# Causal attention beside a ternary FFN: the products with V of two key chunks made in one visit at every second chunk

## The chip, the cores and the metric

The kernel runs on one core of one Trainium2 chip. The metric is the device time of one execution in microseconds (µs). Three runs of the kernel before gave 2402.01, 2408.93 and 2418.55 µs; the median is 2408.93.

## The reference

The input `x` is 4 batches of 2048 tokens with 256 features. It is normalised over the features, and two branches read the result. The attention branch has 16 heads of 16 features, rotary positions on q and k, and a causal mask; the FFN branch (256 to 1024 and back) rounds its weights to three values and ends in a silu. The output is `x` plus the product of the branches.

```
xn  = layernorm(x)
q, k, v = xn @ Wq.T + bq, xn @ Wk.T + bk, xn @ Wv.T + bv     # 16 heads of 16
q, k = apply_rope(q), apply_rope(k)
att = softmax(where(tril, q @ k.T / 4, -inf))
s   = (att @ v) @ Wo.T + bo
g   = silu(gelu(xn @ ternary(W1).T + b1) @ ternary(W2).T + b2)
out = x + s * g
```

## The kernel before, in words

**Tiling.** Queries are taken in 16 blocks of 512 (`blk`; 4 blocks in each batch, `n = blk % 4`), and the heads in 4 groups of 4 (`g`). A group of a block attends to the keys in chunks of 128. Block `n` has `4 * (n + 1)` chunks, called units here and `kb` in the code, so that a group has 4, 8, 12 or 16 units. The last four units of a group lie on the diagonal and are narrower: 512, 384, 256 and 128 queries. In all there are 64 groups and 640 units.

**The three kinds of attention work on TensorE.** They are short visits, and the text names them by letters:
- **M**, in `maxima` (L686): the scores of the *next* group, queries as output rows, two matmuls into two PSUM banks (L704; on the diagonal a mask is added by L717). VectorE then takes the row maxima of each bank, one `tensor_reduce` per bank (L727, or L731). These maxima are needed one group later.
- **S**, in `scores` (L779): the scores of one chunk and one pair of heads (`j` is 0 or 1), transposed, four matmuls (L791, keys first and then the maxima to be taken off) into two neighbouring banks. ScalarE takes the exponentials of both in one instruction (L798) into a buffer `e` of pool `pp`; on the diagonal GpSimd clears what the mask forbids (L802).
- **V**, in `times_v` (L813): the weighted sum with V of one chunk, four heads side by side in four strips of 32 output columns (L815), eight matmul records in the trace, accumulated in PSUM bank 7 over the whole group.

M and S matmuls use the array in halves of 64 rows (`64*128` in the profile), V uses it in strips of 32 columns (`128*32`), and projections, transposes and FFN use it whole (`128*128`).

**The banks.** Seven PSUM banks are handed out in the order in which they were given back (`bank` at L98, `two_banks` at L103, `release` at L113). The handing out is done while the program is written, not on the chip: the next M or S gets the bank whose last user stands furthest back in the program, and on the chip its matmul waits until that user's reduce or exponential has read the bank. `two_banks` takes, of all free neighbouring pairs, the one whose later member is oldest.

**The order of the work** is written out by the loop from L1092 on. For each unit it advances `values` (L772) by two steps with `next(steps)`, and before each step it lets `maxs.to` (L1124, L1127) make M visits in proportion to the work done, about one per step. A step ends at a `yield`. Before the change, a unit is therefore M, S, S, then M, V, where V is that of the chunk before (`pending`). After the second step come, where there are any, one action of `ends` (in the first unit of a group: the last two V of the group before, and the copy of bank 7 to `av_sb`, L842 to L863), parts of the projection of a later block (`proj`) and deferred steps of the block's end (`finish`). The FFN (`feed`, L566) runs between groups.

**The loads.** Keys, queries and values of a group are loaded by the queue of SyncE (L656, L663, L671). The class `Loads` (L615) counts free buffers: 3 for q, 8 for k, 5 for v. A key tile holds 512 keys; a group of block `n` has `n + 1` of them, and while a group is worked on, M needs those of the next one too.

Of the kernel before, what the change touches and what calls it, by code (L numbers as in the profile page):

```python
# [26 lines left out]
GH = H // G  # L27
# [11 lines left out]
def attention_gated_by_ffn(  # L39
# [63 lines left out]
    def two_banks(name):  # L103
        when = {i: k for k, i in enumerate(free_banks)}
        i = min(
            (i for i in when if i + 1 in when), key=lambda i: max(when[i], when[i + 1])
        )
        free_banks.remove(i)
        free_banks.remove(i + 1)
        taken.setdefault(name, []).append([i, i + 1])  # L110
        return psum[:, i : i + 2, :]

    def release(name):  # L113
        free_banks.extend(taken[name].pop(0))
# [36 lines left out]
    sels = [const.tile([P, P], F32R, name=f"sel{j}") for j in range(GH // 2)]  # L151

    xp = ctx.enter_context(tc.tile_pool(name="xp", bufs=1))
    kp = ctx.enter_context(tc.tile_pool(name="kp", bufs=8))
    vp = ctx.enter_context(tc.tile_pool(name="vp", bufs=5))
    qp = ctx.enter_context(tc.tile_pool(name="qp", bufs=3))
    work = ctx.enter_context(tc.tile_pool(name="work", bufs=2))
# [1 line left out]
    small = ctx.enter_context(tc.tile_pool(name="small", bufs=2))  # L159
    yp = ctx.enter_context(tc.tile_pool(name="yp", bufs=2))  # L160
    hp = ctx.enter_context(tc.tile_pool(name="hp", bufs=4))
    pp = ctx.enter_context(tc.tile_pool(name="pp", bufs=4))
    tp = ctx.enter_context(tc.tile_pool(name="tp", bufs=4))

    def setup():
# [449 lines left out]
    class Loads:  # L615


        def __init__(self):
            self.free = {"q": 3, "k": 8, "v": 5}
            self.next = {  # L620
                "q": iter(groups),
                "k": iter([(*x, c) for x in groups for c in range(x[0] % NQ + 1)]),
                "v": iter([(*x, c) for x in groups for c in range(x[0] % NQ + 1)]),
            }
            self.head = {k: next(i) for k, i in self.next.items()}
            self.ahead = {"q": 2, "k": 2, "v": 1}
            self.now = 0
# [144 lines left out]
    def values(blk, g):  # L772

        n = blk % NQ
        mT, q = mTs.pop((blk, g)), qst[blk, g]
        last = (n + 1) * TT - 1
        pending, exs = [], {}

        def scores(kb, j, q0):  # L779
            s2 = two_banks("s2")  # L780
            w = NB - q0

            at = NB - 2 * P if kb == last else 0
            if not at:
                exs[j] = pp.tile([P, 2, NB], F32, tag="e", name="e")
            e = exs[j][:, :, at : at + w]
            for part in range(2):
                for a in range(2):
                    rows = slice(a * ST, (a + 1) * ST)
                    k = kst[blk, g, kb // TT][rows, j, (kb % TT) * P : (kb % TT + 1) * P]  # L790
                    nc.tensor.matmul(  # L791
                        s2[:, a, :w],
                        (k, sels[j][rows, :])[part],
                        (q[rows, j, q0:], mT[rows, q0:])[part],
                        start=(part == 0),
                        stop=(part == 1),
                    )
            nc.scalar.activation(e, s2[:, :, :w], AF.Exp, scale=1.0 / math.sqrt(HD))  # L798
            release("s2")
            if kb >= n * TT:  # L800

                nc.gpsimd.affine_select(  # L802
                    out=e[:, :, :P],
                    in_=e[:, :, :P],
                    pattern=[[0, 2], [1, P]],
                    compare_op=ALU.is_ge,
                    fill=0.0,
                    base=0,
                    channel_multiplier=-1,
                )  # L810
            return e

        def times_v(kb, ex, q0):  # L813
            for h in range(GH):
                nc.tensor.matmul(  # L815
                    av[h * HP : (h + 1) * HP, q0:],
                    vst[blk, g, kb // TT][:, kb % TT, h * VE : h * VE + HP],
                    ex[h // 2][:, h % 2, : NB - q0],
                    start=(kb == 0),
                    stop=(kb == last),  # L820
                )
            if kb % TT == TT - 1:
                vst.pop((blk, g, kb // TT))
                loads.release("v")

        for kb in range(last + 1):
            q0 = max(kb - n * TT, 0) * P
            ex = [scores(kb, j, q0) for j in range(GH // 2)]
            if kb % TT == TT - 1:
                kst.pop((blk, g, kb // TT))  # L830
                loads.release("k")
            yield
            if kb < last:
                while pending:
                    times_v(*pending.pop())
            pending.append((kb, ex, q0))
            yield
        qst.pop((blk, g))

        def end():  # L840
            for chunk in pending:
                times_v(*chunk)  # L842
            av_sb = one.tile([P, NB], F32, tag="av_sb", name="av_sb")
            nc.scalar.copy(av_sb, av)
            if g == 0:
                ys[blk] = yp.tile([P, KC, NB], F32, tag="y", name="y")
                ws[blk] = small.tile([P, H * NB // P], F32, tag="w", name="w")

            tail = blk == NBLK - 1
            for h in range(GH):  # L850
                d = (g * GH + h) * HD
                queue = nc.scalar if tail and g == G - 1 else nc.sync
                queue.dma_start(
                    out=ys[blk][d % P : d % P + HD, d // P, :],
                    in_=av_sb[h * HP : h * HP + HD, :],
                )
                a = (g * GH + h) * P // H
                nc.sync.dma_start(
                    out=ws[blk][a : a + P // H, :],
                    in_=av_sb[h * HP + HD : h * HP + HD + 1, :].rearrange(  # L860
                        "o (a k) -> o a k", a=P // H
                    ),
                )  # L863
            if tail and g >= G - 2:

                if g == G - 2:
                    last_steps.extend(finish(blk))
                for _ in range(last_steps.index(None) if g == G - 2 else len(last_steps)):
                    deferred.append(last_steps.pop(0))
            elif g == G - 1:  # L870
                deferred.extend(finish(blk))

        ends.append(end)
# [193 lines left out]
    with tc.manual_schedule():  # L1067
# [24 lines left out]
        for i, (blk, g) in enumerate(groups):  # L1092
# [22 lines left out]
            if fast:  # L1115
                for k, _ in enumerate(gate):
                    past += slots.pop(0) if k < FC else 0

                    if k % 3 == 2:
                        maxs.to(past / whole)  # L1120
            steps = values(blk, g)
            for u in range(units):
                past += slots.pop(0)
# [84 lines left out]
```

## Time and profile before

| | µs |
|---|---|
| median of three runs | 2408.93 |
| span of the profiled execution (first to last instruction) | 2397.2 |
| profiled execution's own time: 11.2 before the first instruction, and the span | 2408.4 |
| PE (matmuls) busy | 2269.8 (95%) |
| DVE (VectorE) busy | 1620.1 (68%) |
| ACT (ScalarE) busy | 1472.5 (61%) |
| POOL (GpSimd) busy | 886.6 (37%) |
| mean granted TensorE clock | 0.986 of full |

How to read the profile: a matmul's record lasts from its start to the end of its results, and matmuls follow each other faster than that, so PE can be "busy" all the time and still wait. The distance from one start to the next is what a matmul costs in a stream. "PEld" is the load of the stationary operand, which can run ahead of the matmul; a wait for a bank is often shown there. In the list of waits a line reads: who waited, for whom, µs in total, times, and the longest. In the timeline a line reads: start, µs, engine, line, operation, output and inputs, array tiling, moving shape, how many records are merged, and in brackets the idle time before it and who ended it.

### The profile page before, as it was taken

The page shows a single profiled execution, that of the slowest core. Times are in us where ns is not written, and L with a number is a line of the kernel's source. Part 1 is how long each engine was busy: PE and PEld are TensorE (multiplying, and loading weights), DVE is VectorE, ACT ScalarE, POOL GpSimd, SP SyncE. Part 2 cuts the span into 40 slices and gives each one's busy share as a digit, 9 for nine tenths or more (in the row PEclk, how much of TensorE's full clock was granted, in tenths as well). Part 3 has the DMA queues.
Part 4 walks back from the last instruction along what each step waited for, and adds up shares of the span by engine and source line. Part 5 has one row for each costly group of instructions (what it writes and reads, how often), then busy time and mean ns, then how long its engine had stood idle before and what let it go on. Part 6 is the DMA issues. An engine that isn't in the chain of part 4 may idle for free.

```text
span 2397.2 us, 43912 instructions
## 1 busy us (share of the span) xinstructions
PE 2269.8 (95%) x16852; PEld 1222.7 (51%) x16852; DVE 1620.1 (68%) x2910; ACT 1472.5 (61%) x1889; POOL 886.6 (37%) x1262
## 2 busy tenths in 40 slices
PE   5799999999999999999999999999999999999997
PEld 4554545545455455544545454455554545455443
DVE  9656677775556676696636768768663766777881
ACT  4554656656766565765766565565676646566665
POOL 2136343235443535315344542522525453431000
PEclk8889999999999999999999999999999999999998
DMA  7344335234253524234234443412514352442311
GB/s 222 113 135 161 92 127 157 58 104 136 75 165 118 178 86 159 79 91 145 67 127 128 151 142 111 155 56 86 176 58 140 120 179 79 135 140 62 88 46 32
DMA packets 247617, 280.38 MB, mean 117 GB/s; under 512 B 108784, under 2 KB 143728, under 8 KB 247408
## 3 DMA queue, kind: packets, MB, share of 16 engines
q1 hardware_dynamic: 243680, 271.95, 35.7%
q10 hardware_dynamic: 3728, 5.64, 0.7%
q8 instruction: 132, 2.16, 0.4%
q14 instruction: 77, 0.63, 0.1%
HBM read 181.08 MB, written 87.52 MB: 112 GB/s over the span
## 4 chain that ended last, share of the span: by engine, by line
PE 71%; DVE 10%; ACT 7%; POOL 6%; issue 3%; DMA 2%; SPq 1%; ACTq 0%; DVEq 0%; POOLq 0%
PE psum L791 19%; PE psum L815 19%; PE psum L704 14%; PE psum L600 5%; PE psum L513 3%; PE psum L581 3%; DVE mx L727 3%; ACT e L798 3%; DVE mx L731 2%; PE psum L539 2%; PE psum L953 2%; PE psum L717 2%; ACT mT L765 1%; POOL qklo L397 1%; ACT g L608 1%
## 5 line engine op out<-in xcount | busy, mean ns | idle before, releaser
L727 DVE TENSOR_REDUCE mx<-psum 128x1 f32<-128x512 f32 (+1 forms) x2048 | 1258.2, 666 | 497.1 <-PE psum L704 350.1
L798 ACT ACTIVATE e<-psum 128x1024 f32<-128x1024 f32 (+3 forms) x1280 | 1081.3, 894 | 630.4 <-PE psum L791 596.0
L704 PE MATMUL psum<-kst,qst 64*128 64x512 f32 (+3 forms) x2560 | 613.0, 421 | 27.1 <-ACT h L592 9.3
L815 PE MATMUL psum<-e,vg 128*32 128x512 f32 (+3 forms) x5120 | 596.5, 543 | 15.7 <-POOL e L802 15.5
L802 POOL TENSOR_SCALAR_AFFINE_SELECT e<-e 128x256 f32<-128x256 f32 x512 | 208.0, 416 | 1001.0 <-ACT e L798 972.2
L791 PE MATMUL psum<-qst,kst 64*128 64x512 f32 (+3 forms) x2560 | 554.6, 395 | 22.3 <-DVE mx L727 5.7
L704 PEld LDWEIGHTS psum<-kst,qst 64*128 64x128 f32 x2560 | 309.0, 185 | 449.4 <-DVE mx L727 287.9
L791 PE MATMUL psum<-mT,sel 64*128 64x512 f32 (+3 forms) x2560 | 516.8, 370 | 6.0 <-ACT mT L765 3.2
L791 PEld LDWEIGHTS psum<-qst,kst 64*128 64x128 f32 x2560 | 285.1, 185 | 171.9 <-ACT e L798 55.4
L791 PEld LDWEIGHTS psum<-mT,sel 64*128 64x128 f32 x2560 | 273.3, 186 | 43.7 <-ACT mT L765 24.1
L594 POOL TENSOR_TENSOR hl<-h,hh 128x512 fp32r<-128x512 f32 x128 | 164.9, 1298 | 149.9 <-ACT h L592 114.3
L815 PEld LDWEIGHTS psum<-e,vg 128*32 128x32 f32 x5120 | 109.9, 108 | 161.0 <-issue 112.4
L731 DVE TENSOR_REDUCE mx<-psum 128x3 f32<-128x384 f32 x256 | 130.3, 552 | 57.7 <-PE psum L717 53.3
L592 ACT ACTIVATE hh<-psum,b1c 128x512 fp32r<-128x512 f32 x128 | 88.4, 691 | 80.4 <-PE psum L581 80.2
L513 PE MATMUL psum<-xf,wqkvT 128*128 128x512 f32 x256 | 125.9, 616 | 0.9 <-ACT xf L458 0.9
L717 PE MATMUL psum<-mask_k,mask_q 64*128 64x64 bf16 (+1 forms) x1536 | 121.1, 205 | 0.0
L600 PE MATMUL psum<-hh,w2T 128*128 128x512 f32 x256 | 107.1, 418 | 0.2 <-ACT w2T L367 0.2
L581 PE MATMUL psum<-xh,w1T 128*128 128x512 f32 x256 | 104.8, 409 | 0.6 <-POOL xh L396 0.5
L581 PE MATMUL psum<-xl,w1T 128*128 128x512 f32 x256 | 103.1, 403 | 0.8 <-POOL xl L397 0.8
L600 PE MATMUL psum<-hl,w2T 128*128 128x512 f32 x256 | 102.3, 399 | 0.2
L521 ACT ACTIVATE qk<-psum,bqk 128x512 f32<-128x512 f32 x64 | 44.0, 689 | 86.4 <-PE psum L513 85.9
L592 ACT ACTIVATE h<-psum,b1c 128x512 f32<-128x512 f32 x128 | 87.9, 687 | 0.0
(135 smaller groups left out, 1635.9 us busy)
## 6 DMA issues: line engine op xcount, KB each, us to landing
kst<-kd SPq DMA_DIRECT2D x160, 512.0 KB
qst<-qd SPq DMA_DIRECT2D x64, 512.0 KB
vg<-vd SPq DMA_DIRECT2D x160, 166.0 KB
qd<-qkhi SPq DMA_DIRECT2D x32, 512.0 KB
qd<-qklo SPq DMA_DIRECT2D x32, 512.0 KB
kd<-qkhi SPq DMA_DIRECT2D x30, 512.0 KB
kd<-qklo SPq DMA_DIRECT2D x30, 512.0 KB
vd<-v SPq DMA_DIRECT2D x16, 574.0 KB
```

What stands on the lines that cost most here:

```text
L513: nc.tensor.matmul(pq, wqkvT[:, kc, at : at + P], xf[:, kc, :], start=(kc == 0), stop=(kc == KC - 1),)
L581: nc.tensor.matmul(ph, w1T[:, kc, f * P : (f + 1) * P], x12[:, kc, :], start=(kc + i == 0), stop=(kc + i == KC),)
L592: nc.scalar.activation(to, ph, AF.Gelu, bias=b1c[:, f : f + 1])
L600: nc.tensor.matmul(pgs[dc], w2T[:, f - 2, dc * P : (dc + 1) * P], hx, start=(f - 2 + i == 0), stop=(f - 2 + i == FC),)
L704: nc.tensor.matmul(s1[:, at : at + wt], q[rows, j, t * P : (t + 1) * P], kst[blk, g, c][rows, j, :wt], start=(at == 0), stop=(c < n),)
L717: nc.tensor.matmul(to[:, :, i * ST : (i + 1) * ST], mask_q[rows, i, :], mask_k[rows, i, : len(ts), :], start=False, stop=(i == 1),)
L727: nc.vector.tensor_reduce(mx[:, 2 * j + a, at : at + 1], s1[:, :w], AX.X, ALU.max)
L731: nc.vector.tensor_reduce(mx[:, 2 * j + a, at : at + w // P], s1[:, :w].rearrange("p (b k) -> p b k", k=P), AX.X, ALU.max,)
L791: nc.tensor.matmul(s2[:, a, :w], (k, sels[j][rows, :])[part], (q[rows, j, q0:], mT[rows, q0:])[part], start=(part == 0), stop=(part == 1),)
L798: nc.scalar.activation(e, s2[:, :, :w], AF.Exp, scale=1.0 / math.sqrt(HD))
L802: nc.gpsimd.affine_select(out=e[:, :, :P], in_=e[:, :, :P], pattern=[[0, 2], [1, P]], compare_op=ALU.is_ge, fill=0.0, base=0, channel_mult ...
L815: nc.tensor.matmul(av[h * HP : (h + 1) * HP, q0:], vst[blk, g, kb // TT][:, kb % TT, h * VE : h * VE + HP], ex[h // 2][:, h % 2, : NB - q0 ...
```

## The change

Three things are changed.
1. In `values`, V is no longer made in every unit for the chunk before. At every even `kb` the products of both pending chunks are made, one after the other in their order; at an odd `kb` there are none.
2. So that each unit still has two steps, an odd unit gives control back between its two S: its order becomes M, S, M, S. An even unit is M, S, S, then M, V, V.
3. The pool `pp` of the exponentials has six buffers in place of four (4 KB per partition each), and the pool `kp` of the keys six in place of eight (4 KB each); the count in `Loads` follows.

The last two chunks of a group are still made together in the first unit of the next group, and nothing changes in what is computed.

```
-    kp = ctx.enter_context(tc.tile_pool(name="kp", bufs=8))
+    kp = ctx.enter_context(tc.tile_pool(name="kp", bufs=6))
...
-    pp = ctx.enter_context(tc.tile_pool(name="pp", bufs=4))
+    pp = ctx.enter_context(tc.tile_pool(name="pp", bufs=6))
...
-            self.free = {"q": 3, "k": 8, "v": 5}
+            self.free = {"q": 3, "k": 6, "v": 5}
...
         for kb in range(last + 1):
             q0 = max(kb - n * TT, 0) * P
-            ex = [scores(kb, j, q0) for j in range(GH // 2)]
+            ex = [scores(kb, 0, q0)]
+            if kb % 2:
+                yield
+            ex.append(scores(kb, 1, q0))
             if kb % TT == TT - 1:
                 kst.pop((blk, g, kb // TT))
                 loads.release("k")
             yield
-            if kb < last:
+            if kb % 2 == 0:
                 while pending:
-                    times_v(*pending.pop())
+                    times_v(*pending.pop(0))
+                yield
             pending.append((kb, ex, q0))
-            yield
         qst.pop((blk, g))
```

## The prediction

> **What bounds the kernel now.** First the page's busy shares and the chain that ended last:
>
> ```profile
> PE 2269.8 (95%) x16852; PEld 1222.7 (51%) x16852; DVE 1620.1 (68%) x2910; ACT 1472.5 (61%) x1889; POOL 886.6 (37%) x1262
> ...
> PE 71%; DVE 10%; ACT 7%; POOL 6%; issue 3%; DMA 2%; SPq 1%; ACTq 0%; DVEq 0%; POOLq 0%
> ```
>
> TensorE looks like the bound. But a matmul record contains its latency, so the second view is the timeline of PE in a stretch without projections (block with n = 3):
>
> ```profile
> 1392.78 0.86 PE L815 MATMUL psum<-e,vg 128*32 128x256 f32 x16
> 1393.56 0.50 PE L704 MATMUL psum<-kst,qst 64*128 64x512 f32 x2
> 1394.24 0.50 PE L791 MATMUL psum<-qst,kst 64*128 64x512 f32 x2 [0.18 <-ACT e L798]
> ...
> 1396.59 0.50 PE L704 MATMUL psum<-kst,qst 64*128 64x512 f32 x2
> 1397.07 0.51 PE L791 MATMUL psum<-qst,kst 64*128 64x512 f32 x2
> 1397.41 0.40 PE L791 MATMUL psum<-mT,sel 64*128 64x512 f32 x2
> 1397.65 0.39 PE L791 MATMUL psum<-qst,kst 64*128 64x512 f32 x2
> 1397.87 0.40 PE L791 MATMUL psum<-mT,sel 64*128 64x512 f32 x2
> 1398.11 0.39 PE L704 MATMUL psum<-kst,qst 64*128 64x512 f32 x2
> 1398.43 1.07 PE L815 MATMUL psum<-e,vg 128*32 128x512 f32 x8
> 1399.42 0.50 PE L704 MATMUL psum<-kst,qst 64*128 64x512 f32 x2
> ```
>
> One unit is 1396.59 to 1399.42, 2.83 us. By starts: a pair of half-array matmuls costs 0.23 (1397.65 to 1397.87), so M is 0.23 and S 0.46. M costs 0.32 ahead of V (1398.11 to 1398.43) and 0.34 behind it (1399.42 to the next S at 1399.76). V costs 0.99. Without waits a unit is 0.34 + 0.92 + 0.32 + 0.99 = 2.57; 0.26 is waiting, most of it hidden in the records. For whom, the third and fourth views say (waits; then ACT, DVE and PE rows, and the groups by shape):
>
> ```profile
> ACT e L798 <- PE psum L791: 596.0, 604, 4.9
> DVE mx L727 <- PE psum L704: 350.1, 299, 8.5
> PEld psum L704 <- DVE mx L727: 287.9, 433, 3.4
> PEld psum L815 <- POOL e L802: 21.3, 30, 1.6
> ```
>
> ```profile
> 1393.17 1.02 ACT L798 ACTIVATE e<-psum 128x1024 f32<-128x1024 f32 x1
> 1397.91 1.94 ACT L798 ACTIVATE e<-psum 128x1024 f32<-128x1024 f32 x2 [0.89 <-PE psum L791]
> 1423.82 0.73 PE L704 MATMUL psum<-kst,qst 64*128 64x512 f32 x4
> 1424.35 1.29 DVE L727 TENSOR_REDUCE mx<-psum 128x1 f32<-128x512 f32 x2 [5.17 <-PE psum L704]
> L727 DVE TENSOR_REDUCE mx<-psum 128x1 f32<-128x512 f32 x1792 | 1129.6, 683 | 441.6 <-PE psum L704 350.1 <-PE psum L717 73.8 <-PE psum L791 3.1
> L798 ACT ACTIVATE e<-psum 128x1024 f32<-128x1024 f32 x896 | 870.9, 1022 | 401.8 <-PE psum L791 391.2 <-issue 3.7 <-POOL xh L396 2.6
> ```
>
> The reader is to see that each engine waits for the other through the seven banks. S at 1394.24 starts 0.05 after the exponential that read its bank (1393.17 + 1.02 = 1394.19). So a bank comes back at these ages. **A bank of M:** the first reduce starts 0.53 after M (1423.82 to 1424.35), lasts 0.69, the second starts 0.60 later (1.29 - 0.69): with 0.05 for the release the banks are free 1.27 and 1.87 after M's start. **A bank of S:** results are ready when the second pair ends (1397.65 to 1398.27) and the exponential starts 0.1 later, 0.72 after S; 1.02 long, 0.05 release: free 1.79 after S's start.
>
> **What the change takes away.** A group of U units has U - 1 V visits before and U/2 after: 3, 7, 11, 15 become 2, 4, 6, 8, so 576 become 320, 256 fewer. A V visit of 512 columns takes 0.99; the one at 1392.78 holds two chunks of 256 and 128 columns and takes 0.78. So a column costs 0.21/128 = 1.65 ns, a visit 0.15 beside its columns, and two full chunks in one visit 1024 x 1.65 ns + 0.15 = 1.85. With the M before (0.32 for 0.23) and the M behind (0.34 for 0.23) a visit less saves 0.15 + 0.09 + 0.11 = 0.35. All 256: 90 us, the most that PE can win.
>
> The Trainium skill, "TensorEngine Tiling (Array Packing)", says under Key Properties that changing the tiling mode drains TensorE, which is this 0.35; by that alone the time would be 2408 - 90 = 2318. Its section PSUM Bottleneck speaks against: tiling makes TensorE faster but not the emptying of PSUM; by that none of the 90 need arrive. The rows above decide for the second, and the sum below goes by them.
>
> **What it moves.** I followed the list of free banks through both programs. Before, an S nearly always gets a bank with a V between its last user and itself. After, in the 192 full-width odd units that have another odd unit behind them, the second S (S1) gets a bank of the M just ahead of the first S (call it Ma) in 144, and the bank of the first S itself (S0) in 20; only one S and one M, or one M, lie between. In the even unit behind, the second S (S1') gets the bank of S1 in nearly all, with one M and one S between. So two latencies that V used to cover lie bare in each pair of units, while V, V comes as one lump in which DVE and ACT run dry.
>
> Priced from Ma's start at 0: S0 at 0.34, second M (Mb) at 0.80, S1 could start at 1.03. It starts at 1.27 (Ma's first bank), 1.87 (second bank) or 0.34 + 1.79 = 2.13 (S0's). S1' starts 1.79 later at the earliest: 3.06, 3.66 or 3.92; unhindered it would be S1 + 1.15. Where the S before it (S0') gets Mb's second bank, that is free at 0.53 + 3 x 0.60 + 0.69 + 0.05 = 3.07, and S1' comes at 3.53 at the earliest. Behind S1' stand S 0.46, M 0.32 and V, V 1.85: 2.63 to the next Ma. Pairs: 5.69, 6.16, 6.29, 6.55.
>
> *133 full-width pairs without projection work* (measured now: mean 5.84). 31 have first bank and then Mb's second (6.16), 39 second bank (6.29), 20 first bank throughout (5.69), 17 S0's (6.55), 9 no M at all (4.25 as now), 17 other mixtures (6.2): mean 6.05. Now, the commonest sort of pair has a floor near 5.54 and a mean of 5.92, since other work of DVE and ACT (the 0.59 copy to av_sb, sums, statistics) comes between. The new chain runs through the same two engines. Bounds: none of the 0.38 or all, 6.05 to 6.43; I take half, 6.25. So +0.41 x 133 = **+55** (28 to 78).
>
> *59 full-width pairs with projection work* (now 7.79). Work between S1 and the next M covers S1', work behind V, V covers nothing: PE work 4.81 (M 0.92, S 1.84, V 1.85, switches 0.20) and a stall of 0.84, or 6.05, plus the visit; a projection visit of 1.91 gives 7.56 or 7.96 where 7.55 is seen now. 0 to +0.6, I take 0.35: **+21** (0 to 35).
>
> *64 narrow pairs on the diagonal.* The same with shorter reduces (0.55) and exponentials (0.81): some 0.4 x 64 = 26 lost. Against it V waits less for GpSimd's masking, since the chunk just masked is the second of the visit or comes two units later: at most the 21 of the list above, I take 16. **+10** (-15 to 30).
>
> *Buffers.* Six for exponentials suffice: a pair's buffers come back with the V, V ahead of the S that needs them; nothing waits. With six key tiles, the key loads with 8 or more units between issue and first M fall from 138 to 75 of 160, and most of the rest have 4 or 5. Four units are 11 us; 512 KB take 2.3 to 4.5 us at the page's 222 and 117 GB/s. SP's queue can delay them: six come three units behind a store of projections that waits for POOL (up to 9.1 us in SP's waits). 0 to 30, I take **+5**.
>
> FFN, first block and group ends keep their order: 0. Sum: 55 + 21 + 10 + 5 = **+91**; bounds +13 and +173. Against the profiled execution's own 2408.4 (its span 2397.2 and 11.2 ahead; 0.5 under the median of the runs) this makes 2500, between 2421 and 2581.
>
> **Rivals.**
> *TensorE is the bound and wins.* For it: 95% busy, 71% of the chain, and 287.9 us of PEld waits for DVE that a V, V might let DVE catch up with. Against: the ages of the banks. It decides if S1 starts within 0.1 of 1.03 behind Ma. Price: -0.35 x 256 = -90, 2318; with half of it, 2363. Chance 0.10.
> *Both cancel.* If nearly all S1 wait for the first bank only (0.24) and S0' hides the rest, pairs are 5.69 for 5.84: -20 + 21 + 5, about 2415. Chance 0.08.
> *The keys come late.* For it: 4 units of lead where there were 8 or more. If a load took over 11 us, two a group would wait in 16 long groups, some 3 us each: +96 on top, about 2595. Against: 2.3 to 4.5 us. Chance 0.07.
> *The forecast*: 0.75.
>
> **Numbers.** 2500. Faster by over 1% 0.10, within 1% 0.08, slower 0.82; 1% is about what a measurement of this kernel can tell. The range reaches from 2424, above the cancelling case, to 2575: left out are 0.10 + half of 0.08 below and some 0.06 above.
>
> **What would show it.** 320 V visits, the two-chunk ones at 1.85. PE busy falls below 92%, DVE and ACT gain share in the chain. PEld L791 waits for DVE rise from 31.9 us in 59 times to some 80 in over 120, and for ACT from 55.4 in 160 by some 70. V's waits for POOL shrink to a few us. M's waits for the key loads stay under 20. I am wrong if S1 follows Mb at 0.23 in most odd units, if the pairs at full width without projections stay under 5.8, or if DMA waits carry the loss.

## The result and the profile after

The changed kernel takes 2507.06 µs (median of four runs, 2504.78 to 2509.78), against 2407.07 for the kernel before on the same chip: a ratio of 1.0412 with a 95% interval of 1.038 to 1.0443. It is slower by some 100 µs, where +91 (2500) was forecast. The profiled spans are 2502.8 and 2397.2: 105.6 apart. Two of the ten executions of one kernel below (the changed kernel with half maxima) were disturbed, 3880 and 10874 µs; its median leaves them out, and its trace, which is of the first, is not read.

The page of the changed kernel, the lines that answer to those shown of before (busy shares and chain), with the group of the first matmuls of S (keys) of its fifth part, and under it the same group of the kernel before:

```profile
PE 2320.7 (93%) x16852; PEld 1239.3 (50%) x16852; DVE 1601.9 (64%) x2910; ACT 1486.1 (59%) x1889; POOL 882.5 (35%) x1262
...
PE 67%; DVE 15%; ACT 11%; issue 3%; DMA 1%; POOL 1%; SPq 1%; ACTq 0%; DVEq 0%; POOLq 0%
...
L791 PE MATMUL psum<-qst,kst 64*128 64x512 f32 (+3 forms) x2560 | 704.4, 418 | 103.2 <-ACT e L798 53.3
```

```profile
L791 PE MATMUL psum<-qst,kst 64*128 64x512 f32 (+3 forms) x2560 | 554.6, 395 | 22.3 <-DVE mx L727 5.7
```

Two things are to be seen. The chain lost 4 points on PE and gained 5 on DVE and 4 on ACT. And "busy" misleads: PE is busy for 51 µs more with the same 16852 matmuls, because waits that are short enough disappear inside the records: the row at 501.32 below, 1.09 long where 0.39 is usual, holds one. The first matmuls of S were 554.6 µs busy before and are 704.4 now, with 103.2 of visible idle time where there were 22.3.

The list of waits of the changed kernel (who waited, for whom: µs in total, times, longest):

```profile
ACT e L798 <- PE psum L791: 690.4, 612, 7.7
DVE mx L727 <- PE psum L704: 450.0, 299, 6.3
PEld psum L791 <- DVE mx L727: 157.0, 364, 1.7
PEld psum L791 <- ACT e L798: 129.6, 211, 1.4
PEld psum L704 <- DVE mx L727: 114.8, 217, 3.3
PEld psum L815 <- POOL e L802: 17.7, 53, 1.1
PE psum L815 <- POOL e L802: 0.6, 4, 0.2
```

In the list of the kernel before, S (L791) had:

```profile
PEld psum L791 <- ACT e L798: 55.4, 160, 0.8
PEld psum L791 <- DVE mx L727: 31.9, 59, 1.0
```

S now waits for reduces 364 times in place of 59 and for exponentials 211 times in place of 160; ACT and DVE in turn idle 94 and 100 µs more for want of scores. M (L704) waits less for reduces than before, 114.8 µs in place of 287.9.

A pair of units at full width shows how. As in the prediction, Ma, S0, Mb, S1 are the visits of the odd unit, and S0' and S1' the two S of the even unit behind it; Mc is the M between S1 and S0'. The timelines of PE, then DVE and ACT, of the changed kernel, in a group of a block with n = 3:

```profile
500.04 0.50 PE L704 MATMUL psum<-kst,qst 64*128 64x512 f32 x2
500.38 0.39 PE L791 MATMUL psum<-qst,kst 64*128 64x512 f32 x2
...
500.84 0.39 PE L704 MATMUL psum<-kst,qst 64*128 64x512 f32 x2
501.32 1.09 PE L791 MATMUL psum<-qst,kst 64*128 64x512 f32 x2
501.92 0.73 PE L791 MATMUL psum<-mT,sel 64*128 64x512 f32 x2
502.26 0.39 PE L704 MATMUL psum<-kst,qst 64*128 64x512 f32 x1
...
503.12 0.50 PE L791 MATMUL psum<-qst,kst 64*128 64x512 f32 x1 [0.23 <-DVE mx L727]
...
503.82 0.49 PE L791 MATMUL psum<-qst,kst 64*128 64x512 f32 x2
504.16 0.40 PE L791 MATMUL psum<-mT,sel 64*128 64x512 f32 x2
504.39 0.39 PE L704 MATMUL psum<-kst,qst 64*128 64x512 f32 x2
504.71 1.92 PE L815 MATMUL psum<-e,vg 128*32 128x512 f32 x16
506.57 0.49 PE L704 MATMUL psum<-kst,qst 64*128 64x512 f32 x2
```

```profile
500.57 3.68 DVE L727 TENSOR_REDUCE mx<-psum 128x1 f32<-128x512 f32 x6 [1.12 <-PE psum L704]
...
501.10 1.03 ACT L798 ACTIVATE e<-psum 128x1024 f32<-128x1024 f32 x1 [1.96 <-PE psum L791]
502.74 1.03 ACT L798 ACTIVATE e<-psum 128x1024 f32<-128x1024 f32 x1 [0.62 <-PE psum L791]
```

Ma stands at 500.04. The second S of the odd unit (S1) could start at 501.07 and starts at 501.32, its second pair only at 501.92: its two banks are Ma's, and Ma's two reduces end 1.22 and 1.82 after Ma. S0' gets its second bank at 503.12 (the fourth of the six reduces). S1' starts at 503.82, which is 0.05 after the exponential of S1 (502.74 + 1.03 = 503.77). Then V, V takes 1.86 (504.71 to 506.57) as one block. In the V, V just ahead of this pair DVE and ACT had run dry: they stand idle for 1.12 and 1.96 before their first work for it (500.57 and 501.10). The pair lasts 6.53; the same pair of the kernel before lasts 5.85.

**Where the 105.6 µs are.** From the first matmuls of S in both traces, by stretches: 133 plain full-width pairs 5.84 to 6.58 each, +98; 59 full-width pairs with projection work 7.79 to 8.25, +27; the 64 narrow pairs +4; a group's first unit -3; from a group's last unit to the next group -20. The sum is +106.

### The profile page after: what moved, and what is told of

Read it like the earlier page. It is cut to its first block, busy times and chain, and to the rows that moved or that the text cites. A ratio compares the mean times of both kernels' runs of the same rounds, so it can differ in the third digit from the quotient of the medians.

```text
span 2502.8 us, 43871 instructions
## 1 busy us (share of the span) xinstructions
PE 2320.7 (93%) x16852; PEld 1239.3 (50%) x16852; DVE 1601.9 (64%) x2910; ACT 1486.1 (59%) x1889; POOL 882.5 (35%) x1262
## 4 chain that ended last, share of the span: by engine, by line
PE 67%; DVE 15%; ACT 11%; issue 3%; DMA 1%; POOL 1%; SPq 1%; ACTq 0%; DVEq 0%; POOLq 0%
PE psum L815 19%; PE psum L791 18%; DVE mx L727 12%; PE psum L704 10%; ACT e L798 7%; PE psum L600 5%; PE psum L513 5%; PE psum L581 3%; PE psum L539 2%; PE psum L956 2%; PE psum L717 1%; ACT L592 1%; PE psum L455 1%; ACT h L592 1%; ACT hh L592 1%
## 5 line engine op out<-in xcount | busy, mean ns | idle before, releaser
L727 DVE TENSOR_REDUCE mx<-psum 128x1 f32<-128x512 f32 (+1 forms) x2048 | 1243.2, 666 | 622.4 <-PE psum L704 450.0
L798 ACT ACTIVATE e<-psum 128x1024 f32<-128x1024 f32 (+3 forms) x1280 | 1100.1, 896 | 743.9 <-PE psum L791 690.4
L791 PE MATMUL psum<-qst,kst 64*128 64x512 f32 (+3 forms) x2560 | 704.4, 418 | 103.2 <-ACT e L798 53.3
L704 PE MATMUL psum<-kst,qst 64*128 64x512 f32 (+3 forms) x2560 | 602.4, 405 | 32.8 <-ACT e L798 10.7
L791 PE MATMUL psum<-mT,sel 64*128 64x512 f32 (+3 forms) x2560 | 604.0, 382 | 3.7 <-ACT mT L765 3.1
L815 PE MATMUL psum<-e,vg 128*32 128x512 f32 (+3 forms) x5120 | 544.3, 542 | 0.6 <-POOL e L802 0.6
L791 PEld LDWEIGHTS psum<-qst,kst 64*128 64x128 f32 x2560 | 330.9, 186 | 373.0 <-DVE mx L727 157.0
L704 PEld LDWEIGHTS psum<-kst,qst 64*128 64x128 f32 x2560 | 310.0, 186 | 309.0 <-DVE mx L727 114.8
L791 PEld LDWEIGHTS psum<-mT,sel 64*128 64x128 f32 x2560 | 304.5, 187 | 31.8 <-ACT mT L765 17.0
L815 PEld LDWEIGHTS psum<-e,vg 128*32 128x32 f32 x5120 | 135.4, 110 | 248.3 <-issue 206.4
L594 POOL TENSOR_TENSOR hl<-h,hh 128x512 fp32r<-128x512 f32 x128 | 164.7, 1297 | 146.8 <-ACT h L592 114.8
```

Source lines behind the costliest of these rows:

```text
L594: nc.gpsimd.tensor_tensor(hl, h, hh.bitcast(F32), ALU.subtract)
L704: nc.tensor.matmul(s1[:, at : at + wt], q[rows, j, t * P : (t + 1) * P], kst[blk, g, c][rows, j, :wt], start=(at == 0), stop=(c < n),)
L727: nc.vector.tensor_reduce(mx[:, 2 * j + a, at : at + 1], s1[:, :w], AX.X, ALU.max)
L791: nc.tensor.matmul(s2[:, a, :w], (k, sels[j][rows, :])[part], (q[rows, j, q0:], mT[rows, q0:])[part], start=(part == 0), stop=(part == 1),)
L815: nc.tensor.matmul(av[h * HP : (h + 1) * HP, q0:], vst[blk, g, kb // TT][:, kb % TT, h * VE : h * VE + HP], ex[h // 2][:, h % 2, : NB - q0 ...
```

## The experiments

The theory: S and M wait for banks, because two latencies (reduce and exponential) that one V in each unit used to cover lie bare. The rivals: the keys come late; the split of the odd unit alone does the harm; the lump of two V alone does it; an engine's throughput, not the time that banks are held.

### The buffers alone

The kernel before with six key tiles and six exponential buffers:

```
-    kp = ctx.enter_context(tc.tile_pool(name="kp", bufs=8))
+    kp = ctx.enter_context(tc.tile_pool(name="kp", bufs=6))
-    pp = ctx.enter_context(tc.tile_pool(name="pp", bufs=4))
+    pp = ctx.enter_context(tc.tile_pool(name="pp", bufs=6))
-            self.free = {"q": 3, "k": 8, "v": 5}
+            self.free = {"q": 3, "k": 6, "v": 5}
```

> The order of work of before, with only the pools of the change: six key tiles and six exponential buffers. Theory (banks): nothing waits for key loads even with four units of lead, so the time is that of before, ratio 0.995 to 1.005. Rival (keys come late): two loads a group wait in the long groups and the time rises by 20 us or more, ratio above 1.008.

Measured: 2403.93 against 2407.65, ratio 0.9991 (0.9977 to 1.0005). The key buffers cost nothing, and neither in this run nor in the changed kernel does TensorE wait for a key load in any line of the waits. That rival is out.

### The merged visit without the split

```
-            if kb < last:
+            if kb % 2 == 0:
                 while pending:
-                    times_v(*pending.pop())
+                    times_v(*pending.pop(0))
+            yield
             pending.append((kb, ex, q0))
-            yield
```

(with the changed kernel's pools; both S of a unit stay together)

> V of two chunks in one visit at every second unit, but the odd unit is not split: M, S, S, M, then M, S, S, M, V, V. Theory (banks): with no V in the odd unit the first S of the even unit waits for the exponential of the second S of the odd unit, with only two M between: from the M that opens the odd unit, S is at 0.34 and 0.80, the second exponential ends at 0.34 + 0.72 + 0.92 + 1.02 = 3.00, so S comes at 3.05 where it could come at 1.72; then 0.92, 0.32 and 1.85: 6.14 a pair against 5.5 to 5.9 now. With 133 plain pairs at +0.3 to +0.5 and less elsewhere the time is 2440 to 2500, ratio 1.015 to 1.04. Rival (the split of the odd unit does the harm, the merged visit pays its 0.35 each): 2320 to 2380, ratio below 0.99.

Measured: 2494.21, ratio 1.036 (1.0336 to 1.0384). The merged visit alone costs most of the loss, though each visit removed should save TensorE its 0.35. In the waits S hangs on ACT, as reckoned, and hardly more on DVE than before:

```profile
PEld psum L791 <- ACT e L798: 137.7, 234, 1.1
PEld psum L791 <- DVE mx L727: 32.3, 69, 1.1
```

### The split without the merged visit

```
-            ex = [scores(kb, j, q0) for j in range(GH // 2)]
+            ex = [scores(kb, 0, q0)]
+            if kb % 2:
+                yield
+            ex.append(scores(kb, 1, q0))
             if kb % TT == TT - 1:
                 kst.pop((blk, g, kb // TT))
                 loads.release("k")
-            yield
+            if kb % 2 == 0:
+                yield
```

> The odd unit is split (M, S, M, S, V), V stays one chunk in each unit, pools as before. Theory (banks): the second S of an odd unit still gets a bank of the M that opens the unit (144 of 192 full-width units) or of the first S (20), so it comes at 1.27, 1.87 or 2.13 in place of 1.03, while V now covers the wait of the even unit's second S; 0.2 to 0.6 a pair: 2440 to 2510, ratio 1.015 to 1.045. Rival (only the lump of two V lets ACT and DVE run dry, the split is harmless): 2400 to 2420, ratio 0.995 to 1.005.

Measured: 2464.86, ratio 1.0232 (1.0212 to 1.0253). The split alone costs 57 µs, and here it is mostly the other wait that grows:

```profile
PEld psum L791 <- DVE mx L727: 105.0, 243, 1.7
PEld psum L791 <- ACT e L798: 71.8, 151, 1.4
```

So neither part is harmless. The merge lays the exponential bare, the split the reduce; together they do not add (87 and 57 alone, 100 in one). That a wait for one covers part of the other would explain this; it was not measured by itself.

### Banks held for a shorter time

If it is the time for which banks are held, shortening the reduces and exponentials must take the loss away. Each cut is made in the changed kernel and in the kernel before, and the two are compared with each other. The cut in the maxima (second half of the columns only) leaves half of the keys out of the maxima; the cut in the exponentials takes the first half of the queries and lets V read that half twice, so that TensorE's work stays.

```
-                            mx[:, 2 * j + a, at : at + 1], s1[:, :w], AX.X, ALU.max
+                            mx[:, 2 * j + a, at : at + 1], s1[:, w // 2 : w], AX.X, ALU.max
...
-            nc.scalar.activation(e, s2[:, :, :w], AF.Exp, scale=1.0 / math.sqrt(HD))
+            we = w // 2 if w > 2 * P else w
+            nc.scalar.activation(
+                e[:, :, :we], s2[:, :, :we], AF.Exp, scale=1.0 / math.sqrt(HD)
+            )
...
+                    to = to.rearrange("p (a k) -> p a k", a=2)
+                    p = p[:, : w // 2].unsqueeze(1).to_broadcast([P, 2, w // 2])
```

Maxima only, the changed kernel:

> The changed kernel with the row maxima taken over the second half of the columns only (the maxima leave out half of the keys; everything else is as it was). A reduce of 256 columns should last 0.42 (0.683 at 512 and 0.549 at 384), so a bank of M is free at 1.00 and 1.33 in place of 1.27 and 1.87; a bank of S is still free at 1.79. Theory (banks): pairs of 5.45, 5.75 or 6.55, some 0.3 above those of the kernel before with the same cut; 45 to 75 us between the two, where uncut there are 100. Rival (the loss is VectorE's throughput): the loss goes wholly, under 20 us. Rival (the loss has nothing to do with how long banks are held): still 90 to 110 us.

and its standard, the kernel before:

> The kernel before with the same cut (maxima over half of the columns), the standard for the run above. The plain pair is held by ScalarE's chain (two exponentials, then the next S), so it gains little: 2360 to 2400 us by every theory.

Both cuts, the changed kernel and its standard:

> The changed kernel with half maxima and, in units of 384 and 512 queries, exponentials of the first half of the queries only; V reads that half twice, so TensorE's work is unchanged (the exponentials of the other queries are left out, which changes the result). An exponential then lasts 0.60 in place of 1.02 and a bank of S is free at 0.72 + 0.60 + 0.05 = 1.37. Theory (banks): S1 at 1.03 to 1.33, S1' 1.37 behind it where 1.15 is unhindered, pairs of 5.0 to 5.3 against a TensorE floor of 4.81; the kernel before with the same cut lies near its own floor of 5.14. So the loss of 100 us against that one goes to between -40 (faster) and +20. Rival (the merged visit or the new order costs TensorE itself): the loss stays above 60.

> The kernel before with half maxima and half exponentials, the standard for the run above. Pairs near 5.14 to 5.3 where they are 5.5 to 5.9: 133 plain pairs at -0.5 and some less in the others: 2300 to 2360 us.

Exponentials only, the changed kernel and its standard:

> The changed kernel with full maxima, and exponentials of the first half of the queries in units of 384 and 512 queries (V reads that half twice; the other exponentials are left out, which changes the result). Of the loss of 100 us 29 were left with half maxima and -17 with both cuts; if the two latencies add, this cut alone leaves 100 - (29 + 17) = 54 against the run below. Theory (banks): 35 to 75. If it is ScalarE alone that holds the new order, under 20.

> The kernel before with half exponentials and full maxima, the standard for the run above. The exponential's chain, which gives the plain pair its floor of 5.54, gets 0.8 shorter, so VectorE and TensorE hold the pair next: 2320 to 2370 us.

| cut | changed kernel | kernel before | difference |
|---|---|---|---|
| none | 2507.06 | 2407.07 | +100 |
| half maxima | 2407.57 | 2378.48 | +29 |
| half exponentials | 2458.51 | 2378.08 | +80 |
| both | 2288.38 | 2305.09 | -17 |

(Ratios to the uncut kernel before, in the order of the cuts: changed kernel 1.0004, 1.0233 and 0.9501; before 0.9861, 0.9894 and 0.9565; each interval within ±0.006.) A reduce of 256 columns lasted 0.42, and an exponential of half the queries 0.60, in the profiles of the cut kernels. V still takes 0.996 for one chunk and 1.854 for two in them, as without the cuts.

With both latencies short the total changes sides: the changed kernel is then 17 µs faster. Where this comes from, the traces show by stretches (changed kernel minus kernel before, from the first matmuls of S, in µs):

| stretch | no cut | half exponentials | both |
|---|---|---|---|
| 192 full-width pairs | +125 | +96 | +28 |
| 64 narrow pairs | +4 | +8 | -17 |
| first units of the groups | -3 | -2 | -2 |
| last unit of a group to the next group | -20 | -19 | -19 |

The two cuts take 97 of the 125 µs that the full-width pairs lose, so most of that loss does hang on the time for which banks are held. But these pairs are still 28 µs slower, and S still waits for exponentials more than in the kernel before with the same cuts (L799 is the exponential here; first the kernel before, then the changed one):

```profile
PEld psum L791 <- ACT e L799: 20.2, 34, 0.8
PEld psum L791 <- ACT e L799: 73.1, 196, 1.0
```

Whether these waits are all of the 28 was not taken apart. The change of sign comes from elsewhere: from the groups' ends, where the changed kernel wins 19 to 20 µs whatever is cut, and from the narrow pairs, where it wins 17 with both cuts. V's waits for GpSimd are then 20 µs shorter than in the kernel before (20.1 for 39.8), so that not even there is the saving in visits seen by itself. No run shows the 0.35 a visit in the time of the full-width pairs.

The cut in the maxima leaves 29: not the 45 to 75 of the theory, and not the under 20 of the rival in which VectorE's throughput is everything. The cut in the exponentials leaves 80 and not 35 to 75. So the reduces weigh more than I reckoned. The loss falls by 71, by 20 and by 117 with both, more than the sum; that each chain is covered by the other would explain it. VectorE's throughput is not the cause by itself, since with VectorE's work cut the exponentials still hold 46 (from +29 to -17), and both kernels give VectorE and ScalarE the same number of instructions (2910 and 1889). Two expectations failed beside: the kernel before with half exponentials was to come to 2370 at most and took 2378, and with both cuts the plain pairs were to last 5.0 to 5.3 in the changed kernel and 5.14 to 5.3 in the one before; they last 5.54 and 5.36 by the mean. That the difference of -17 lies inside its range of -40 to +20 is therefore luck.

### One bank less in the kernel before

```
-    free_banks = list(range(7))
+    free_banks = list(range(6))
```

> The kernel before with six banks handed out in place of seven; the order of work is untouched. If the number of banks against their age is what holds TensorE, one bank less shortens every distance between two users of a bank, and also the order of before must wait: 2450 to 2530 us. Rival (the order of before has banks to spare, and only the new order asks for more): 2400 to 2420.

Measured: 2657.38, ratio 1.1058 (1.1032 to 1.1084), 250 µs more than before, twice what the upper end of the reckoning allowed. The order of before does not have banks to spare either. In its waits it is M that shows it, a visit that I had not priced at all:

```profile
PEld psum L704 <- DVE mx L727: 252.5, 729, 3.7
PEld psum L704 <- ACT e L798: 250.5, 315, 0.8
```

The kernel before has 287.9 µs in 433 times and 14.8 in 31 in these two lines: what has grown is M's wait for exponentials. How much of the 254 µs it makes was not taken apart.

### Keeping the gain at the groups' ends

From a group's last unit to the next group the changed kernel gains 20 µs. The first attempt kept the order of before and let V come two units behind its scores on the diagonal:

```
-            if kb < last:
-                while pending:
-                    times_v(*pending.pop())
+            while len(pending) > (1 if kb > n * TT else 0):
+                times_v(*pending.pop(0))
```

> The order of before down to the diagonal; on the diagonal V comes two units behind its scores in place of one (no V in the second diagonal unit, one in the last), with the six buffers of each kind. It is meant to keep what the changed kernel gained at the groups' ends (20 us less from the last unit of a group to the next group, fewer waits of V for GpSimd) without its order elsewhere. Theory: V's waits for GpSimd (37 us in the two lines of the waits) mostly go, but the unit without V lays a bank wait of up to 0.8 us bare in each of 64 groups: 2385 to 2425, ratio 0.99 to 1.007. Rival: GpSimd's masking was hidden anyway, and only the bare wait is seen: 2420 to 2450.

Measured: 2403.10, ratio 0.9979 (0.9966 to 0.9992). V's waits for GpSimd do go (21.3 and 15.5 µs before, 3.3 and 1.5 here), but the time does not go with them. By stretches the narrow pairs are 33 µs shorter and the way from a group's last unit to the next group is 34 longer, since a V has moved from the one into the other. In the waits of the kernel before, the matmuls that turn the maxima (L757) read:

```profile
PEld psum L757 <- DVE m_pad L748: 17.5, 33, 0.9
PE psum L757 <- DVE m_pad L748: 12.8, 33, 0.8
```

Here the first line stays (17.7 µs in 28 times) and the second is gone. In the changed kernel neither is left: its V, V ahead of a group's last unit, by the prediction's prices 0.85 longer than the one V there before, covers the last reduce and the three small VectorE steps behind it. It is the merged visit that does this and not the split: from the last unit to the next group the kernel before takes 419 µs in all, the merged visit alone 398, the split alone 420. So the second attempt takes the changed order on the diagonal only, from the second diagonal unit to the last:

```
+            split = kb > n * TT and kb % 2
+            ex = [scores(kb, 0, q0)]
+            if split:
+                yield
+            ex.append(scores(kb, 1, q0))
...
-            if kb < last:
+            if not split:
                 while pending:
-                    times_v(*pending.pop())
+                    times_v(*pending.pop(0))
+                yield
             pending.append((kb, ex, q0))
-            yield
```

> The order of before down to the diagonal, and the changed order (split odd unit, one visit for two chunks) only in the second to fourth unit of the diagonal; buffers of the change. Theory: between the last unit of a group and the next group the changed kernel gained 20 us, since the longer V visit covers the last reduce and the turning of the maxima, and its narrow pairs lost 4 us, so 2407 - 16 = 2391 us, 2380 to 2400, ratio 0.989 to 0.997. Rival (that gain was only the other side of waits in the full-width units): 2400 to 2412.

Measured: 2397.44 against 2408.15, ratio 0.9953 (0.9935 to 0.9972): inside the range of ratios, some 11 of the 16 µs. By stretches the 20 at the groups' ends are there, but the narrow pairs lose 8 and not 4, and the full-width pairs lose 6 though their order is that of before; why they do was not taken apart. This version is half a per cent faster than the kernel before.

## Why the prediction was right

The direction, the size (+91 forecast, +100 measured) and the mechanism held: S waits for banks, and the full-width pairs lose; shorter reduces and exponentials take away 97 of the 125 µs lost there, and what holds the other 28 stays open. That the sum came so near is partly luck. By stretches the traces differ by 106: plain pairs lose 43 more than forecast and pairs with projections 6 more; against that stand 20 at the groups' ends, 6 in the narrow pairs, 5 for buffers and 3 in the first units.

- **What the change takes away.** There are 320 V visits; two full chunks take 1.854 in 192 of them (forecast 1.85). Beside two single visits of 0.996 that is 0.14 saved in the visit itself (0.15 forecast). That the whole 0.35 a visit, 90 in all, would show in the time was given as a bound; no run shows it.
- **The ages of the banks** came out to the hundredth. In plain pairs, by the median and from Ma: first reduce 0.53, second reduce's end 1.82, S0's exponential 1.06, Mb's second reduce's end 3.02; every release 0.05.
- **Plain pairs: +55 forecast, +98 measured**, beyond the 78 given as this term's upper bound. The mis-sized term is the price of the pairs: 5.69, 6.16, 6.29 and 6.55 were reckoned, medians of 6.25, 6.34, 6.53 and 6.87 were measured from Ma to Ma. After a stop the first pair of an S takes 0.34 and not 0.23, as 503.82 to 504.16 shows; two stops in a pair make 0.22 of the 0.24 between 6.29 and 6.53. In the sort reckoned at 5.69 (20 pairs without other work) S1' comes at 3.18 and not 3.06, because S1's exponential has to wait on ScalarE until S0's ends (2.09); the stop adds 0.11; and in 8 of the 20 the M behind S1' waits for Mc's first reduce until 4.20, some 0.45. M had been priced as if it never waited.
- **Pairs with projections: +21 forecast, +27 measured.**
- **Narrow pairs: +10 forecast, +4 measured.** V's waits for GpSimd fell less than I said on one line (21.3 to 17.7) and wholly on the other (15.5 to 0.6).
- **Buffers: +5 forecast, nothing measured.**
- **"Group ends keep their order: 0"** was wrong by 20 µs. No V stands in this stretch in either kernel, but the visit just ahead of the last unit is longer, and it covers the tail of the maxima, a wait that stood in the list of waits of before (L757, 30 µs in its two lines).
- **Signs named in advance.** S's waits for ACT rose from 55.4 to 129.6 (some 70 more were named); for DVE to 157.0 in 364 times, where 80 in over 120 were named. V's waits for GpSimd shrank to 18, not to a few. The sign against me, S1 behind Mb at 0.23, is there in half: S1's first matmul comes within 0.3 of Mb in 86 of the 171 full-width odd units with an M just ahead of S1, since it needs only one of the two banks; the second matmul does so in 7. PE busy fell to 93%, not below 92%: waits shorter than a record's latency count as busy.

The rival in which TensorE is the bound fell with the merged visit alone (1.036); late keys fell with the buffers alone. Of the two sayings of the Trainium skill's page "TensorEngine Tiling (Array Packing)", the drain at a change of tiling mode (Key Properties) agrees with the rows here, which price a visit less at 0.35; still it is the one on emptying PSUM (PSUM Bottleneck) that fits the time: fewer visits did not make the kernel faster, and the full-width pairs lose 28 µs in place of 125 when reduces and exponentials are made shorter.

## What to carry to other kernels

Before work is gathered into longer visits of one engine, write down for each buffer which visit used it last and what stands between: work that looks like overhead may be the cover of another engine's latency, and a "95% busy" engine may be waiting inside its records. Here the longer visit paid only at the end of a group, where it covered the tail of another chain, and cost time elsewhere. To see whether an operation holds a new order, shorten it in both versions and compare the two with each other, by stretches and not by their totals alone: a total can change its sign for reasons that have nothing to do with the suspect.

## What the runs showed that I had not expected

- One PSUM bank less cost the kernel before 10.6%, more than the whole change.
- A stop can cost more than its length. In the changed kernel, all 51 full-width S behind another S whose first pair starts 0.6 µs or more after the last matmul ahead take 0.34 µs for that pair; none of the 72 that start within 0.3 does (0.23).
- The merged visit alone costs 3.6% and the split alone 2.3%, both together 4.1%: the costs of the two halves do not add, and neither do the gains when the two latencies are cut.
